# A second level of Strassen's algorithm for one of seven products, and layer-0 row sums on ScalarE

## The chip, the cores and the metric

The kernel runs on one NeuronCore of a Trainium2 chip. TensorE (PE) multiplies matrices into eight PSUM banks, VectorE (DVE) and ScalarE (ACT) work elementwise and empty the banks, GpSimd (POOL) does elementwise work on SBUF alone, and SyncE (SP) issues DMAs. The metric is the device time of the program in microseconds. Three runs of the kernel before gave 1717.29 to 1717.60, median 1717.36.

## The reference

x is 64 batch elements of 256 tokens by 512 features in float32; adj is a 256 x 256 matrix of zeros and ones.

```python
# layer 0
h = relu(layernorm(x))
q, k, v = h @ Wq.T, h @ Wk.T, h @ Wv.T
rel = adj.T * (q @ k.T)                       # per batch element
rel = rel / norm(rel, axis=2, keepdims=True)  # rows over m
x = x + rel @ v
# layer 1
h = relu(layernorm(x))
x = x + (adj @ h) @ weight + bias
```

## The kernel before, in words

Two batch elements make a pair: 512 token rows, held as four chunks of 128 rows. There are 32 pairs, and five input buffers are used in turn. Wq and Wk are multiplied into one matrix M before the pairs start, so a pair needs these products: g (h times M), v (h times Wv), scores (g against h), attend (rel times v), gather (adj times the second h) and mix (times `weight`).

All but the gather use the seven-product (Winograd) form of Strassen's algorithm: each operand is a 2 x 2 grid of blocks, sums of blocks are made by DVE (`left_factors`, lines 158 to 161, and `right_operands`, lines 133 to 136), and seven block products take the place of eight. The products run in the order one, five, six, three, seven, two, four, in three PSUM banks: bank_a takes 1, 6, 7 and 4, bank_c takes 5 and 3, bank_b takes 2. After each product a "take" adds the bank to a block of the result. A first take into g, v or rel is a copy by ACT; all other takes are DVE adds. A block product of g, v or mix is four matmuls of 256 columns, one of the scores four of 128 columns, one of the attend two of 256. An fp32 matmul stands in the trace as two records.

`steady(i)` is the loop body, run for 28 of the 32 pairs; `first_pairs` and `last_pairs` are the ends. It runs in this order on PE: attend of pair i, its seven products alternating with the seven v products of pair i+1 (`attend_and_v`); scores of pair i+1; g of pair i+2 (`project_g`); gather of pair i; mix of pair i. Between products the other engines' work is handed in by "slots": slot n is what is run after the n-th product and its take. On PE, DVE and ACT the program's order is kept as it is written; [...]the slots set each queue's order.

What else matters around the change:

- Layer-0 statistics of pair i+3 (`norm`, lines 248 and 249: two DVE instructions for each chunk) run in the attend slots, then a square root on ACT, two small DVE instructions, and four Relu on ACT (line 260) that write h.
- h is turned in two steps. `place_blocks` issues 16 DMAs on SP's queue (line 299) that permute 32 x 32 blocks from h into the tile `blocks`; then eight DVE transposes (line 309) make ht. In the kernel before they stand in the gather's slots. `sums` are the four DVE operand sums of ht.
- rel is turned likewise. In the slots of g the masks, squares (line 380), root, inverse and scales run, then `place` issues 16 DMAs on SP's queue (line 396) from rel into `placed`, and four DVE transposes (`turns`, line 399, slot 4 of mix) make `turned`. Their sums (`rel_steps`, slot 5 of mix) and those of v (`v_steps`) are the operands of the next attend.
- Layer 1: statistics of the attended x on DVE (`halves`), Relu on ACT, and a split of h into a rounded part (`upper`, ACT, line 499) and the rest (`lower`, DVE, line 503), because the gather runs in the fp32r form, once with each part. POOL adds the bias to x (line 495) and stores each finished pair.

Of the kernel before, what the change touches and what calls it, by code (L numbers as in the profile page):

```python
# [9 lines left out]
F32 = mybir.dt.float32  # L10
# [9 lines left out]
def kernel(  # L20
# [60 lines left out]
    X, H, HL, G, V, R, H2, Y = ({} for _ in range(8))  # L81
# [12 lines left out]
    adj_sb = const.tile([P, NC, N], F32, name="adj_sb")  # L94
# [48 lines left out]

    def run(steps):
        for step in steps:
            step()
# [5 lines left out]
    def left_factors(a, s):  # L152

        v = nc.vector
        steps = [
            lambda: v.tensor_sub(s[0], a(0, 0), a(1, 0)),
            lambda: v.tensor_add(a(1, 0), a(1, 0), a(1, 1)),
            lambda: v.tensor_sub(s[1], a(1, 0), a(0, 0)),  # L160
            lambda: v.tensor_sub(s[2], a(0, 1), s[1]),
        ]
        return {1: a(0, 0), 2: a(0, 1), 3: s[2], 4: a(1, 1), 5: a(1, 0), 6: s[1], 7: s[0]}, steps
# [29 lines left out]

    def winograd(product, take, side={}, early=False):

        for at, step in enumerate(winograd_steps(product, take, early)):
            step()
            run(side.get(at, ()))
# [66 lines left out]


    def ln0(i):

        if i == 0:
            H[i] = blocks.rearrange("p c d e -> p c (d e)")  # L270
        else:
            H[i] = work.tile([P, TC, D], F32, tag="hy", name=f"h_{i}")
        h = H[i]
        chunks, root, end, relu = norm(flat(X[i]))
        return chunks, root, end, [(lambda c=c: relu(h[:, c, :], c)) for c in range(TC)]

# [3 lines left out]
    def transposes_by_matmul(i):  # L280
        h, ht = H.pop(i), new_ht(i)
        for d in range(DC):
            pt = ps_m.tile([P, T], F32, tag="pm", name="pt")
            for half in range(NC):
                for b in range(NB):
                    nc.tensor.transpose(
                        pt[:, ts(half * NB + b, P)], h[:, b * NC + half, ts(d, P)], ident
                    )
            nc.scalar.copy(ht[:, d].rearrange("p h t -> p (h t)"), pt)
        HL[i], sums = left_operands(twice, ht, "hs", i)  # L290
        return sums

# [23 lines left out]
    def project_g(i, side={}):  # L316

        g = work.tile([P, DC, NC, HT_], F32, tag="g", name=f"g_{i}")

        def take(t, k, bank, first):  # L320
            dst = g[:, k * HC : (k + 1) * HC, t, :]
            src = bank.rearrange("p (e t) -> p e t", e=HC)
            if first:
                nc.scalar.copy(dst, src)  # L324
            else:
                nc.vector.tensor_add(dst, src, dst)

        winograd(product_tokens_moving(HL[i], m_right), take, side)
        G[i] = g

    def g_operands(i, tag="ys"):

        g, t = G[i], work.tile([P, 3, HC, HT_], F32, tag=tag, name=f"gt_{i}")
        G[i], steps = right_operands(
            lambda j, k: g[:, j * HC : (j + 1) * HC, k], [t[:, n] for n in range(3)]
        )
        return steps
# [16 lines left out]

    def scores(i, side={}, by_matmul=False):
# [6 lines left out]
        square = work.tile([P, N], F32, tag="square", name=f"square_{i}")  # L362
# [16 lines left out]
        def square_sum(b, k):  # L379
            nc.scalar.activation(square, rel[:, b, k], AF.Square, accum_out=rn[:, b, k : k + 1])  # L380
# [62 lines left out]
    def attend_operands(i):  # L443


        turned, rel = R.pop(i)
        v, t = V.pop(i), work.tile([P, 3, NB, HD], F32, tag="gt", name=f"vt_{i}")
        room = rel.rearrange("p b k m -> p (b k m)")
        left, left_steps = left_factors(
            lambda n, m: turned[:, :, m, n],  # L450
            [room[:, ts(j, HT_)].rearrange("p (b n) -> p b n", b=NB) for j in range(3)],
        )
        right, right_steps = right_operands(
            lambda m, k: v[:, :, m, ts(k, HD)], [t[:, n] for n in range(3)]
        )
        R[i] = left, right
        return right_steps, left_steps

    def attend_and_v(i, side):
# [14 lines left out]
        both = zip(winograd_steps(product, take), winograd_steps(*v_products(i + 1)))  # L474
        for at, (step, v_step) in enumerate(both):
            step()
            v_step()
            run(side.get(at, ()))
# [31 lines left out]
    def gather(i, exact, side={}):  # L510
        h2 = H2.pop(i)
        if exact:
            terms = [(h2[:, s], adjt_r[:, m, :], m) for m in range(NC) for s in range(2)]
        else:
            terms = [(h2, adjt_sb[:, m, :], m) for m in range(NC)]
        y = work.tile([P, DC, NC, NB, P], F32, tag="hy", name=f"yt_{i}")
        for b in range(NB):
            for d0 in range(0, DC, 2):
                pm = ps_m.tile([P, 2, N], F32, tag="pm", name="py")
                for d in range(2):  # L520
                    for n, (left, right, m) in enumerate(terms):
                        nc.tensor.matmul(  # L522
                            pm[:, d, :], left[:, b * NC + m, ts(d0 + d, P)], right,
                            start=(n == 0), stop=(n == len(terms) - 1),
                        )
                nc.scalar.copy(  # L526
                    y[:, d0 : d0 + 2, :, b, :], pm.rearrange("p d (h n) -> p d h n", h=NC)
                )
                run(side.get(b * 2 + d0 // 2, ()))
        Y[i], steps = left_operands(work, y.rearrange("p d h b n -> p d h (b n)"), "ys", i)  # L530
        return steps

    def mix(i, side={}, early=False):
# [10 lines left out]
        winograd(product_weights_moving(Y.pop(i), w_right), take, side, early)  # L544
# [11 lines left out]
    def layer_1(parts):  # L556
# [4 lines left out]
            1: [uppers[0], uppers[1], lowers[0]],  # L561
            2: [relus[2], lowers[1]],
            3: [relus[3], uppers[2], uppers[3]],
# [4 lines left out]
    def before_pairs():  # L568
# [42 lines left out]
        def take(t, k, bank, first):  # L611
# [15 lines left out]
            4: [transpose_wv, end] + relus + [right_steps[3]],  # L627
            5: m_steps[0:3],
# [11 lines left out]
    w_right, w_steps = weight_operands(w_sb, "w")  # L640
    in_order = {EngineType.PE, EngineType.DVE, EngineType.Activation}
# [7 lines left out]
    def pairs(exact):  # L649
        with tc.manual_schedule(engines=in_order):  # L650
            sums = first_pairs(exact)
            for i in range(1, NP - 3):
                if i + 4 < NP:
                    load(i + 4)
                sums = steady(i, exact, sums)
            last_pairs(exact, sums)

    def first_pairs(exact):
# [35 lines left out]
            3: turned2[4:6] + relus[2:4], 4: turned2[6:8], 5: turns[0:2], 6: turns[2:4],  # L694
# [3 lines left out]
            0: sums2[0:1], 1: sums2[1:2], 2: sums2[2:3], 6: sums2[3:4],  # L698
# [6 lines left out]
        if exact:  # L705
# [5 lines left out]
        y_steps = gather(0, exact, {  # L711
            0: turned3[4:8], 1: v_steps[0:1], 2: v_steps[1:3], 3: v_steps[3:4],
        })
        run(y_steps[0:2])
        mix(0, {0: y_steps[2:3], 1: y_steps[3:4], 4: turns, 5: rel_steps})
        return sums3

    def steady(i, exact, sums):
# [4 lines left out]
        stats0, root0, end0, relus0 = ln0(i + 3)  # L723
        stats, root, end, relus, uppers, lowers = ln1(i, exact)
        halves = [stats[b * NC + t] for t in range(NC) for b in range(NB)]
        attend_and_v(i, {
            0: stats0[0:2], 1: stats0[2:4] + [root0], 2: [end0, relus0[0]] + gs[0:2],
            3: relus0[1:2] + gs[2:3], 4: relus0[2:3] + gs[3:4], 5: relus0[3:4] + sums[0:1],
            6: halves[0:2],
        })  # L730
        place_blocks(i + 3)
        masks, squares, norm_root, inverse, scales, place, turns = scores(i + 1, {
            0: halves[2:3], 1: halves[3:4] + [root], 2: [end] + sums[1:2], 3: relus[0:1],
            4: relus[1:2], 5: uppers[0:1], 6: uppers[1:2] + sums[2:4],
        })
        v_steps, rel_steps = attend_operands(i + 1)
# [3 lines left out]
            2: uppers[2:4] + squares[0:2] + v_steps[0:1],  # L740
            3: lowers[2:3] + squares[2:4] + [norm_root],
            4: lowers[3:4] + [inverse] + scales + [place],
            5: v_steps[1:2],
            6: v_steps[2:4],
        })
        turned, sums = transpose_blocks(i + 3)
        y_steps = gather(i, exact, {0: turned[0:3], 1: turned[3:6], 2: turned[6:8]})
        run(y_steps[0:2])
        mix(i, {0: y_steps[2:3], 1: y_steps[3:4], 4: turns, 5: rel_steps})
        return sums  # L750

    def last_pairs(exact, sums):
# [5 lines left out]
        attend_and_v(a, {  # L758
# [14 lines left out]
        gs = g_operands(c, "gt")  # L773
# [13 lines left out]
        attend(c, {n: [stats[n], y_steps[n]] for n in range(TC)}, rn)  # L787
        mix(b, layer_1(parts))
# [39 lines left out]
```

## Time and profile before

| | |
|---|---|
| Median of three runs | 1717.36 us |
| Profiled execution | 1717.2 us, span 1715.1 us |
| PE busy | 1702.2 us, 99% of the span |
| DVE busy | 1360.1 us, 79% |
| ACT busy | 663.3 us, 39% |
| POOL busy | 201.2 us, 12% |
| Granted TensorE clock | 0.999 |

The span runs from the first to the last instruction of the profiled execution; the execution's own time is 2.1 us longer. Busy time is the union of an engine's records. Matmuls overlap one another, so the mean duration of a record (380 ns for 256 columns) is longer than the distance between two records; the chain that ended last gives the distance. A line of the waits reads: engine, tile and line that waited, what released it, microseconds in total, times, and the longest. A line of the groups gives the operation with its operands, how often it ran, then the busy time and the mean duration of one in nanoseconds, then the idle time before it.

### The profile page before, as it was taken

The page shows a single profiled execution, that of the slowest core. Times are in us where ns is not written, and L with a number is a line of the kernel's source. Part 1 is how long each engine was busy: PE and PEld are TensorE (multiplying, and loading weights), DVE is VectorE, ACT ScalarE, POOL GpSimd, SP SyncE. Part 2 cuts the span into 40 slices and gives each one's busy share as a digit, 9 for nine tenths or more (in the row PEclk, how much of TensorE's full clock was granted, in tenths as well). Part 3 has the DMA queues.
Part 4 walks back from the last instruction along what each step waited for, and adds up shares of the span by engine and source line. Part 5 has one row for each costly group of instructions (what it writes and reads, how often), then busy time and mean ns, then how long its engine had stood idle before and what let it go on. Part 6 is the DMA issues. An engine that isn't in the chain of part 4 may idle for free.

```text
span 1715.1 us, 24952 instructions
## 1 busy us (share of the span) xinstructions
PE 1702.2 (99%) x9170; PEld 1518.2 (89%) x9170; DVE 1360.1 (79%) x2672; ACT 663.3 (39%) x1387; POOL 201.2 (12%) x167
## 2 busy tenths in 40 slices
PE   9999999999999999999999999999999999999998
PEld 7979998989898999889898989998889989899986
DVE  6778888878888888888787888888888888887655
ACT  4434433444333344334443333443343433334331
POOL 0011100111101111001111011110011110011111
PEclk9999999999999999999999999999999999999999
DMA  7423333233332233332233322333322334222011
GB/s 239 65 33 80 77 86 76 51 59 80 81 86 66 45 74 77 86 77 56 53 81 80 87 67 48 71 76 85 78 59 49 81 80 87 68 53 41 28 24 63
DMA packets 425972, 122.34 MB, mean 71 GB/s; under 512 B 398064, under 2 KB 399344, under 8 KB 425840
## 3 DMA queue, kind: packets, MB, share of 16 engines
q1 hardware_dynamic: 413248, 80.28, 25.1%
q0 software_dynamic: 8432, 32.51, 5.0%
q10 hardware_dynamic: 4160, 7.87, 1.3%
q8 instruction: 74, 1.21, 0.3%
q14 instruction: 58, 0.48, 0.1%
HBM read 38.27 MB, written 33.55 MB: 42 GB/s over the span
## 4 chain that ended last, share of the span: by engine, by line
PE 96%; DVE 3%; ACT 0%; DMA 0%; issue 0%; ACTq 0%; DVEq 0%
PE bank_a L217 25%; PE bank_c L217 13%; PE bank_a L205 13%; PE py L522 7%; PE bank_a L229 7%; PE bank_b L217 7%; PE bank_c L205 6%; PE bank_a L465 6%; PE bank_c L229 3%; PE bank_b L205 3%; PE bank_c L465 3%; PE bank_b L229 2%; PE bank_b L465 1%; DVE st L248 1%; PE pu L430 0%; DMA wk_sb<-in_L_gnn_Wk_dram 0%
## 5 line engine op out<-in xcount | busy, mean ns | idle before, releaser
L346 ACT COPY v<-bank_a 128x512 f32<-128x512 f32 x96 | 56.2, 586 | 676.6 <-PE bank_a L217 676.6
L495 POOL TENSOR_TENSOR x_ring<-x_ring,bias_bc 128x512 f32<-128x512 f32 x128 | 176.3, 1396 | 822.6 <-DVE rel L372 548.8
L248 DVE BATCH_NORM_STATS2 st<-x_ring 128x6 f32<-128x512 f32 x256 | 171.5, 670 | 0.4
L539 DVE TENSOR_TENSOR x_ring<-bank_a,x_ring 128x512 f32<-128x512 f32 x128 | 88.2, 689 | 57.9 <-PE bank_a L217 57.9
L522 PE MATMUL py<-adjt_r,h 128*128 128x256 f32 x1024 | 130.4, 285 | 0.0
L522 PEld LDWEIGHTS py<-adjt_r,h 128*128 128x128 f32 x1024 | 123.9, 189 | 1.6
L217 PE MATMUL bank_a<-w_t,ys 128*128 128x256 f32 x512 | 121.3, 380 | 1.7 <-DVE x_ring L539 1.7
L217 PE MATMUL bank_a<-wv_t,hs 128*128 128x256 f32 x512 | 121.0, 379 | 0.0
L205 PE MATMUL bank_a<-hs,m_t 128*128 128x256 f32 x512 | 121.0, 379 | 0.0
L260 ACT ACTIVATE h2c<-x_ring,nb,rs 128x512 f32<-128x512 f32 x128 | 100.6, 810 | 32.6 <-DVE h L503 25.9
L217 PEld LDWEIGHTS bank_a<-w_t,ys 128*128 128x128 f32 x512 | 95.7, 190 | 17.3 <-DVE x_ring L539 3.0
L217 PEld LDWEIGHTS bank_a<-wv_t,hs 128*128 128x128 f32 x512 | 97.4, 190 | 13.1
L205 PEld LDWEIGHTS bank_a<-hs,m_t 128*128 128x128 f32 x512 | 97.4, 190 | 13.1
L546 POOL DMA_DIRECT2D out_dram<-x_ring x31 | 24.0, 773 | 671.2 <-issue 489.2
L503 DVE TENSOR_TENSOR h<-h2c,h 128x512 fp32r<-128x512 f32 x128 | 91.1, 711 | 5.6 <-ACT h L499 5.6
L526 ACT COPY yt<-py 128x512 f32<-128x512 f32 x128 | 75.1, 587 | 47.2 <-PE py L522 47.2
L260 ACT ACTIVATE h<-x_ring,nb,rs 128x512 f32<-128x512 f32 x124 | 91.0, 806 | 1.5 <-DVE nb L257 1.5
L309 DVE STREAM_TRANSPOSE ht<-blocks 128x256 f32<-128x256 f32 x248 | 84.8, 407 | 1.4 <-DMA blocks<-h 1.4
L539 DVE TENSOR_TENSOR x_ring<-bank_c,x_ring 128x512 f32<-128x512 f32 x64 | 44.2, 691 | 46.1 <-PE bank_c L217 46.1
L472 DVE TENSOR_TENSOR x_ring<-bank_a,x_ring 128x512 f32<-128x512 f32 x116 | 79.4, 685 | 1.3 <-PE bank_a L465 1.3
L499 ACT CAST h<-h2c 128x512 fp32r<-128x512 f32 x128 | 75.3, 616 | 0.0
L324 ACT COPY g<-bank_a 128x512 f32<-128x512 f32 x96 | 56.2, 586 | 43.2 <-PE bank_a L205 41.1
(175 smaller groups left out, 3669.4 us busy)
## 6 DMA issues: line engine op xcount, KB each, us to landing
blocks<-h SPq DMA_DIRECT2D x496, 64.0 KB, 2.3
out_dram<-x_ring POOLq DMA_DIRECT2D x31, 1024.0 KB, 4.7
x_ring<-in_x_dram SPq DMA_DIRECT2D x28, 1024.0 KB, 5.3
placed<-rel SPq DMA_DIRECT2D x496, 32.0 KB, 2.0
x_ring<-in_x_dram ACTq DMA_DIRECT2D x4, 1024.0 KB, 5.3
wq_sb<-in_L_gnn_Wq_dram SPq DMA_DIRECT2D x4, 256.0 KB, 5.0
wk_sb<-in_L_gnn_Wk_dram ACTq DMA_DIRECT2D x4, 256.0 KB, 6.3
wv_sb<-in_L_gnn_Wv_dram ACTq DMA_DIRECT2D x1, 1024.0 KB, 5.4
```

The lines of the kernel that those rows point to most:

```text
L205: nc.tensor.matmul(bank[:, e * HT_ : (e + 1) * HT_], right[n][:, d, ts(e, P)], left[n][:, d, :], start=(start and e == 0 and d == 0), stop ...
L217: nc.tensor.matmul(bank[:, b * HD : (b + 1) * HD], left[n][:, d, ts(b, P)], right[n][:, d, :], start=(start and b == 0 and d == 0), stop=( ...
L229: nc.tensor.matmul(bank[:, ts(b, P)], right[n][:, d, ts(b, P)], left[n][:, d, ts(b, P)], start=(start and b == 0 and d == 0), stop=(d == H ...
L248: nc.vector.bn_stats(st[:, c, :], src[:, c, :])
L260: nc.scalar.activation(dst, src[:, c, :], AF.Relu, bias=nb[:, c : c + 1], scale=rs[:, c : c + 1])
L309: nc.vector.transpose(ht[:, d, half].rearrange("p (b n) -> p b n", b=NB), by_half[:, :, half, d])
L465: nc.tensor.matmul(bank[:, ts(b, HD)], left[n][:, b], right[n][:, b], start=(start and b == 0), stop=True, skip_group_check=True,)
L472: nc.vector.tensor_add(dst, bank.rearrange("p (b e) -> p b e", b=NB), dst)
L495: nc.gpsimd.tensor_tensor(xt[:, c, :], xt[:, c, :], bias_bc, ALU.add)
L503: nc.vector.tensor_sub(dst[:, 1, c, :], whole_h[c], dst[:, 0, c, :].bitcast(F32))
L522: nc.tensor.matmul(pm[:, d, :], left[:, b * NC + m, ts(d0 + d, P)], right, start=(n == 0), stop=(n == len(terms) - 1),)
L539: nc.vector.tensor_add(xt[block], bank.rearrange("p (b e) -> p b e", b=NB), xt[block])
```

## The change

1. **A second level for one product.** In g, v and mix of the steady pairs, product 2 (which went to bank_b) is itself computed by seven products. Its blocks, 256 x 256 each, are cut once more into 128 x 128, so that seven matmuls of 128 columns stand in place of four of 256. They run in one further bank, `bank_d`, in three 128-column regions, as four groups: 1 and 5 behind product six; 6 and 3 behind three; 7 and 2 behind seven; 4 behind a "spacer". DVE adds the regions to the result: two adds behind group 1, one behind group 2, two behind group 3 (the last with 256 columns), one behind group 4.
2. **Spacers.** Group 4 follows something else on PE: in v the attend product that stands there anyway, in g the first of four gather steps, in mix the first attend product of the next pair.
3. **Operands of the second level.** Twelve 128-column right sums are made once (`second_right`); for each pair four left sums of h (`second_of_h`) and four of y (`second_of_y`). In `left_factors` the sum goes to a fourth room if one is given.
4. **Layer-0 statistics by ScalarE** in the steady pairs (`norm_by_scalar`): a Copy with a row sum and a Square with a bias and a row sum for each chunk, with three small DVE instructions and the root between.
5. **Rooms.** The sums of v (`vt`) lie in the tile `blocks` (`spare_blocks`); the squares' unused output goes to `placed`; the input adj shares the room of `placed`.
6. **Moves.** The transposes of h go from the gather's slots to slots 2 to 5 of g; the sums of ht from the end of `attend_and_v` and the scores to slots 1 to 3 of `attend_and_v`; the sums of g to slots 4 to 6; two of the v sums and two of the rel sums (`late`) into slots 0 and 1 of the next `attend_and_v`. At the ends: `transpose_wv` one slot later, the v sums of pair 1 from the gather into mix, two y sums of the last pairs from attend into mix, and the layer-1 steps of `layer_1` in another order.

```diff
+    def second_level(matmul, add):
+        bank = ps_m.tile([P, 512], F32, tag="pm", name="bank_d")
+        at_a, at_b, at_c = (bank[:, ts(r, P)] for r in range(3))
+        def group_1():
+            matmul(at_a, 1, True)
+            matmul(at_c, 5, False)
+            add(0, 0, at_a)
+            add(1, 1, at_c)
+        def group_2():
+            matmul(at_a, 6, False)
+            matmul(at_c, 3, False)
+            add(0, 1, at_a)
+        def group_3():
+            matmul(at_a, 7, False)
+            matmul(at_b, 2, False)
+            add(1, 1, at_a)
+            add(0, None, bank[:, P : 3 * P])
+        def group_4():
+            matmul(at_a, 4, False)
+            add(1, 0, at_a)
+        return group_1, group_2, group_3, group_4
+    def two_level_steps(product, take, matmul, add, spacer):
+        one, five, six, three, seven, _, four = winograd_steps(product, take)
+        groups = second_level(matmul, add)
+        return [
+            lambda: run([one]),
+            lambda: run([five]),
+            lambda: run([six, groups[0]]),
+            lambda: run([three, groups[1]]),
+            lambda: run([seven, groups[2]]),
+            lambda: run([spacer, groups[3]] if spacer else [groups[3]]),
+            lambda: run([four]),
+        ]
...
+    def norm_by_scalar(src, scratch):
...
+        def total(c):
+            nc.scalar.activation(scratch[:, c, :], src[:, c, :], AF.Copy, accum_out=sm[:, c : c + 1])
+        def mean():
+            nc.vector.tensor_single_scalar(sm, sm, -1.0 / D, op=ALU.mult)
+        def square(c):
+            nc.scalar.activation(
+                scratch[:, c, :], src[:, c, :], AF.Square, bias=sm[:, c : c + 1],
+                accum_out=sq[:, c : c + 1],
+            )
...
+    def spare_blocks():
+        room = blocks.rearrange("p c d e -> p (c d e)")
+        return [room[:, ts(n, 512)].rearrange("p (a b) -> p a b", a=2) for n in range(3)]
...
-        v, t = V.pop(i), work.tile([P, 3, NB, HD], F32, tag="gt", name=f"vt_{i}")
+        v, t = V.pop(i), spare_blocks()
...
-    def steady(i, exact, sums):
+    def steady(i, exact, sums, attends, late, first_done):
...
-        attend_and_v(i, {
-            0: stats0[0:2], 1: stats0[2:4] + [root0], 2: [end0, relus0[0]] + gs[0:2],
-            3: relus0[1:2] + gs[2:3], 4: relus0[2:3] + gs[3:4], 5: relus0[3:4] + sums[0:1],
-            6: halves[0:2],
+        attend_and_v(i, first_done, attends, {
+            0: late[0:3] + totals[0:2], 1: late[3:4] + totals[2:4] + [mean] + sums[0:1],
+            2: row_squares[0:2] + sums[1:3], 3: row_squares[2:4] + [root0, end0] + sums[3:4],
+            4: relus0[0:2] + gs[0:1], 5: relus0[2:4] + gs[1:3], 6: gs[3:4] + halves[0:1],
         })
...
-            2: uppers[2:4] + squares[0:2] + v_steps[0:1],
-            3: lowers[2:3] + squares[2:4] + [norm_root],
-            4: lowers[3:4] + [inverse] + scales + [place],
-            5: v_steps[1:2],
-            6: v_steps[2:4],
-        })
+            2: uppers[2:4] + squares[0:2] + turned[0:2],
+            3: lowers[2:3] + squares[2:4] + [norm_root] + turned[2:4],
+            4: lowers[3:4] + [inverse] + scales + [place] + turned[4:5],
+            5: turned[5:8],
+        }, second=True, spacer=y_products[0])
+        v_steps, rel_steps = attend_operands(i + 1)
+        run_steps(y_products[1:], {0: v_steps[0:1], 1: v_steps[1:2]})
         run(y_steps[0:2])
-        mix(i, {0: y_steps[2:3], 1: y_steps[3:4], 4: turns, 5: rel_steps})
-        return sums
+        y_second = second_of_y(i)
+        attends = attend_steps(i + 1)
+        mix(i, {
+            0: y_steps[2:3], 1: y_steps[3:4] + y_second[0:2], 2: y_second[2:4],
+            4: turns, 5: rel_steps[0:2],
+        }, spacer=attends[0])
+        return sums, attends, v_steps[2:3] + rel_steps[2:4] + v_steps[3:4]
```

## The prediction

> **What bounds the kernel now.** I read the page's busy times and chain first, then the chain in order of time over one steady pair (a pair is 2 of the 64 batch elements; the loop body runs for 28 of the 32), then PE's waits, then the same pair on DVE and SP.
>
> ```profile
> PE 1702.2 (99%) x9170; PEld 1518.2 (89%) x9170; DVE 1360.1 (79%) x2672; ACT 663.3 (39%) x1387; POOL 201.2 (12%) x167
> PE 96%; DVE 3%; ACT 0%; DMA 0%; issue 0%; ACTq 0%; DVEq 0%
> PE bank_a L217 <- DVE x_ring L539: 1.7, 3, 0.9
> PE bank_c L217 <- DVE yt L159: 1.4, 1, 1.4
> ```
>
> PE is the bound, and it waits for hardly anything (all its listed waits add to about 7 us). The time is PE's work, so work taken off PE pays in full, and any new PE wait costs in full. From the chain, in order of time (start, duration, record):
>
> ```profile
> 820.60 0.86 PE bank_a L465 x4
> 823.19 0.89 PE bank_a L229 x8
> 829.44 1.73 PE bank_a L205 x8
> 838.08 1.73 PE bank_b L205 x8
> 841.53 3.77 PE py L522 x32
> ```
>
> An fp32 matmul is two records. 256 columns take 1.727/8 = 215.9 ns a record, 128 columns 0.893/8 = 111.7 ns. One pair on PE: 21 weight products x 1.727, 7 score products x 0.893, 7 attend products x 0.864 and the gather 3.77 = 52.3 us.
>
> DVE and SP of the same pair (start, duration):
>
> ```profile
> 852.60 0.69 DVE L539 TENSOR_TENSOR x_ring<-bank_c,x_ring 128x512 f32<-128x512 f32 x1 [1.38 <-PE bank_c L217]
> 854.33 0.69 DVE L539 TENSOR_TENSOR x_ring<-bank_a,x_ring 128x512 f32<-128x512 f32 x1 [1.03 <-PE bank_a L217]
> 854.93 1.41 DVE L399 STREAM_TRANSPOSE turned<-placed 128x256 f32<-128x256 f32 x4
> 856.27 0.65 DVE L539 TENSOR_TENSOR x_ring<-bank_b,x_ring 128x512 f32<-128x512 f32 x1
> 816.31 11.88 SPq L299 DMA_DIRECT2D blocks<-h  x16
> 841.26 11.34 SPq L396 DMA_DIRECT2D placed<-rel  x16
> blocks<-h SPq DMA_DIRECT2D x496, 64.0 KB, 2.3
> placed<-rel SPq DMA_DIRECT2D x496, 32.0 KB, 2.0
> ```
>
> The row at 854.33 takes product "seven" of the mix; right behind it DVE makes the four `turned` blocks of the next attend. PE first reads them at 857.58, after products "two" and "four". The first block is ready at 854.93 + 0.40 = 855.33: a margin of 2.25 us. The 16 `placed` DMAs start at 841.26 and, at 0.709 apiece plus 2.0 to land, end near 853.9, 1.0 before the turns.
>
> Rows for prices:
>
> ```profile
> L326 DVE TENSOR_TENSOR g<-bank_b,g 128x512 f32<-128x512 f32 x32 | 22.1, 689 | 10.2 <-PE bank_b L205 10.2
> L372 DVE TENSOR_TENSOR rel<-bank_b,rel 128x256 f32<-128x256 f32 x32 | 13.6, 425 | 14.5 <-PE bank_b L229 14.5
> L260 ACT ACTIVATE h<-x_ring,nb,rs 128x512 f32<-128x512 f32 x124 | 91.0, 806 | 1.5 <-DVE nb L257 1.5
> L380 ACT ACTIVATION_READ_ACCUMULATOR square<-rel 128x1 f32 x128 | 24.0, 187 | 0.0
> ```
>
> **What the skill says.** The Trainium skill, "TensorE: Matmul & The Clock Gate", section Back-to-back issue gap: N/2.4 + 2.5 ns. Two passes give 111.7 ns at N = 128, exactly the trace, and 218 at 256 against 215.9. "VectorE: DVE Perf Modes", section The TRN2 errata, prices an fp32 tensor_tensor at (N+151)/0.96 ns: 691 and 424 agree with 689 and 425; for N = 128, which the trace lacks, 291. "ScalarE: Activation LUTs", section What ACT_TABLE_LOAD costs: 186 + 0.833 N ns and 93 for each pointer operand: 799 for the Relu, measured 806. "PSUM — Partial Sum Buffer", section PSUM bank collisions raise a hardware error, has two engines take turns on one bank; no trace here shows a collision, but it is why the second level must run in groups, with DVE's adds between them and PE waiting.
>
> **The change, part by part.** (a) PE. One product of eight records (1.727) becomes seven 128-column matmuls, 14 x 111.7 = 1.564: 0.163 saved. In the loop g, v and mix have it: 0.49 a pair; with one more v behind the loop, 13.8 us in all. This is the whole gain.
>
> (b) DVE, a pair: three takes of 689 go, twelve adds of 291 and three of 425 come: +2.7. Second left operands, 8 x 291: +2.3. The layer-0 statistics, 4 x (670+182), go: -3.4; a scaled mean, +0.2. Net +1.8 on 42.5, still 83% of 53 us, so DVE is not the bound as a sum; where its queue stands at each PE need decides.
>
> (c) ACT: four Copies (613+187) and four Squares with a bias pointer (706+187): +6.8 on 20.7, off the path as a sum. In the attend slots two of them (about 1.5 with overlap) stand between v copies that come every 2.59 us: hidden with 0.5 to spare. But DVE's variance and reciprocal now sit in its queue waiting for ACT's fourth square and root, and the takes of "seven" behind them. Laying the order out with the rows' durations, DVE leaves these 0.2 us before the take would hold PE: hidden, and every 0.1 beyond costs 0.1 a pair (2.8 us).
>
> (d) The spacer in mix. Group 4 needs group 3's add, so attend's first product is put between, directly behind group 3. That product's stationary operand is `turned`. PE now wants it 0.447 us (four small matmuls) after "seven", not 3.45 (two products): 3.01 earlier. DVE does two more adds, about 0.20 + 0.34 in back-to-back spacing, before it turns: 0.54 later. The margin becomes 2.25 - 3.01 - 0.54 = **-1.3 us: a PE stall in each of 28 pairs**. Both matmuls of the product need a turn, but the second is 0.33 behind and PE spends 0.43 on the first. After a stall the first weight load is exposed: the stall at 850.57 made the next product 1.83 instead of 1.73, so +0.1.
>
> (e) Behind it stands a second floor. From "seven" of g to the spacer PE now runs 0.447+0.942+0.223+1.727+2.826+5.180+0.447+1.727+0.447+1.727+0.447 = 16.1 us. `place` came 3.2 after that "seven"; two more adds make it 3.7, and 15 x 0.709 + 2.0 + 0.40 for one turn give 16.75. So the DMAs alone would hold PE about 0.6; now hidden under the 1.3 of (d).
>
> (f) Groups 4 of v and g. From "seven": DVE starts 0.2 later, takes 0.60, adds 0.20 + 0.42, signal 0.04: 1.46. PE has 0.447 + 0.864 (attend product) in v, 0.447 + 0.942 (one gather step) in g: stalls of 0.15 and 0.07. In g, ACT's copy of "five" stands behind a relu that waits for DVE; I put 0.15 on "three".
>
> (g) `vt` moves into `blocks`. Its last reader is attend's last product, so `place_blocks` starts there (about 16 us into the stretch, not 10.5), and needs 15 x 0.742 + 2.3 = 13.4: blocks at about 29.5. The turns of h, moved from the gather to g's slot 2, come at about 30.0: 0.5 to spare on DVE and 1.2 more before PE. Costs nothing while this holds. On SP's queue they end near 28, before `place` at 36.7; POOL's queue (bias adds, the store) is not moved. The squares that now write into `placed` stand ahead of `place` on ACT anyway, and their region's last readers, the turns, are half a pair behind: nothing. Moved too, at nothing while DVE has room: two `v` and two `rel` steps (2.2 us) behind the next v's "one", needed only by attend "six" two products later.
>
> (h) Outside the loop: the shift of transpose_wv and of operand steps may remove the 1.7 and 1.4 waits above: -3 us. The once-made right operands, 12 x 291 = 3.5, lie beside full PE slots.
>
> **Sum.** Per pair -0.49 + 1.3 + 0.1 + 0.15 + 0.07 + 0.15 = +1.28; x 28 = +36; less 0.16 and 3: **+33 us**. The profiled execution took 1717.2 (span 1715.1), within 0.2 of the median 1717.36: 1750.
>
> **Rivals.**
> 1. *The DMAs of `placed` bind the spacer* (e later than d). Speaks for it: only 0.5 us between the two; every delay of DVE in g's slots 3 and 4 shifts `place`. Against: the issue rate is steady in the trace. One microsecond late makes the stall 1.8: +14, 1764.
> 2. *DVE's or ACT's queue holds PE elsewhere*: statistics on ACT slower than their price, or a 128-column add dearer than 291. Slacks in (c) and (f) are 0.2 and below zero, so 0.06 more on each of some 20 small operations costs 0.4 to 0.5 a pair: 1763; 0.2 more, 1810.
> 3. *Shorter stalls*: a 128-column add between 172 (the 128x4 rows) and 291 and quicker signals: stall 1.0, (f) gone, net +0.6: 1734.
> 4. *Faster*: the spacer does not wait. Place: first attend product in mix. It decides at a stall of 0.49 us, below which the gain in (a) wins; with none, 1717.2 - 13.8 - 3 = 1700. It needs the turns 1.3 earlier, or PE already that late for another reason; against it speak both (d) and (e), each enough alone.
> 5. *PE gains nothing*, if seven weight loads with 128 columns each ran slower: the scores (111.7 a record, a new weight each) speak against; then 1764.
>
> **How the numbers follow.** Likeliest, 0.5: 1750, 1738 to 1762. Rival 1: 0.17; rival 2: 0.16; rival 3: 0.10; rival 5: 0.02; rival 4: 0.04; within 0.2% of before, 0.01 (the place where 3 and 4 meet). Leaving out rival 4, the dear end of 2 and the far tails gives 1733 to 1782. Three runs spread 0.3 us, so 0.2% (3.4 us) is about what can be told from no change: faster 0.04, same 0.01, slower 0.95.
>
> **What would show it.** PE's waits should list the attend product (its first bank in mix) behind DVE `turned`, 28 times, about 1.3 each, or behind DMA `placed` if rival 1 holds. The small products should space at 111.7 a record and PE's busy time fall by 14. Waits on the second-level bank should be near 0.15. PE idle of about 50 us would confirm the sum; no such wait, or the turns ahead of the take of "seven", would make it wrong; ht waiting for DMA `blocks` over 1 us would mean (g) failed.

## The result and the profile after

Four runs of the changed kernel gave 1760.72 to 1761.66 us, median 1760.95, against 1717.36 before. The ratio is 1.0254, with a 95% interval of 1.0237 to 1.0272. The change makes the kernel 43.6 us slower. The profiled execution took 1761.66 us, with a span of 1759.4; before, the span was 1715.1, so the two traces differ by 44.3 us, at the same granted clock (0.999).

The page of the kernel after, busy times and the shares of the chain that ended last:

```profile
PE 1711.0 (97%) x9680; PEld 1525.2 (87%) x9680; DVE 1393.6 (79%) x3141; ACT 791.4 (45%) x1835; POOL 192.2 (11%) x167
PE 92%; DVE 4%; SPq 1%; issue 1%; DMA 1%; ACT 0%; DVEq 0%; ACTq 0%
```

PE is still the bound, but it now stands idle for 48.4 us of the span (before: 12.9), and DVE carries 4% of the chain. PE's busy time rose by 8.8 us although its work fell. A record of 256 columns lasts 379 ns and the next one starts 216 ns behind it, so a wait of up to 0.16 us leaves no gap between the records, and a longer one shows 0.16 too short; that part counts as busy. So neither the busy times nor the list of waits gives the whole loss. The list of PE's waits, kernel after:

```profile
PE bank_a L612 <- DVE turned L546: 36.8, 28, 1.4
...
PE bank_d L487 <- DVE ys L169: 0.3, 1, 0.3
```

One wait comes in every one of the 28 pairs, 1.31 us each: the first attend product of the next pair, which is the spacer in mix, waits for the transposes that make `turned`. Of the second-level bank the list has a single wait, 0.3 us.

How long is one pair? The first and last start of attend's product in bank_b give it (29 attends, 28 intervals). Kernel before, then kernel after (durations min/median/max, then first and last start):

```profile
L465 PE MATMUL bank_b<-v,turned x116: 378/379/380, 137.4 to 1603.6; 128*128 128x256 f32 x116
```

```profile
L612 PE MATMUL bank_b<-v,turned x116: 379/379/382, 138.3 to 1650.5; 128*128 128x256 f32 x116
```

(1603.6 - 137.4)/28 = 52.36 before and (1650.5 - 138.3)/28 = 54.01 after: +1.65 a pair, +46 in the loop. The head became 0.9 longer, and the tail (span less the last start) went from 111.5 to 108.9. The sum is +44.3, the whole difference. (The last start is that of the fourth record of its product, 0.65 us behind the first, so every period in this document is 0.02 too long; differences between kernels are not touched.)

Where the 1.65 sits is seen in the chain in order of time over one pair of the kernel after (start, duration, record):

```profile
887.77 0.45 PE bank_d L487 x4
...
895.16 0.49 PE bank_d L487 x2
...
915.39 0.43 PE bank_d L440 x2
...
925.47 0.62 PE bank_d L487 x4
...
930.03 0.48 DVE x_ring L703
...
930.64 0.07 DVE x_ring L491
...
930.84 0.41 DVE x_ring L491
931.25 0.36 DVE turned L546
...
931.75 1.10 PE bank_a L612 x4
932.85 0.22 PE bank_d L487 x2
```

The first line is a group of four small records that waits for nothing: 0.45. A group 4 with nothing to wait for takes 0.22, as in the last line. Against these, group 4 of v takes 0.49, group 4 of g 0.43, and group 1 of mix 0.62. From 930.03 on PE is out of the chain: DVE takes product "seven", adds the two regions of group 3, makes the first turned block, and only then the spacer runs. It stands in the chain with 1.10, where an attend product is 0.86.

DVE, PE and SP at that place (start, duration, line, operation, count, and in brackets the idle time before and what ended it):

```profile
930.03 0.69 DVE L703 TENSOR_TENSOR x_ring<-bank_a,x_ring 128x512 f32<-128x512 f32 x1 [1.28 <-PE bank_a L276]
930.64 0.61 DVE L491 TENSOR_TENSOR x_ring<-bank_d,x_ring 128x128 f32<-128x128 f32 x2
931.17 1.41 DVE L546 STREAM_TRANSPOSE turned<-placed 128x256 f32<-128x256 f32 x4
931.75 1.10 PE L612 MATMUL bank_a<-v,turned 128*128 128x256 f32 x4 [1.31 <-DVE turned L546]
896.59 11.61 SPq L406 DMA_DIRECT2D blocks<-h  x16
917.73 10.39 SPq L543 DMA_DIRECT2D placed<-rel  x16
```

The `placed` DMAs were issued from 917.73, 10.39/16 = 0.65 us apiece, so by estimate the last landed near 917.73 + 15 x 0.65 + 2.0 = 929.5. The turns began 1.7 later and did not wait for it. DVE was idle for 1.28 us before the take of "seven", and in the last 0.5 of these the blocks lay ready; its order held the turns behind the take.

The rows that answer to the price rows of before, from the groups of the kernel after, shapes kept apart, and from its DMA issues:

```profile
L449 DVE TENSOR_TENSOR g<-bank_d,g 128x128 f32<-128x128 f32 x140 | 36.5, 278 | 20.5 <-PE bank_d L440 20.5
L340 ACT ACTIVATE h<-x_ring,sm 128x512 f32<-128x512 f32 x112 | 79.5, 714 | 0.0
L340 ACT ACTIVATION_READ_ACCUMULATOR h<-x_ring,sm 128x1 f32 x112 | 21.4, 191 | 0.0
blocks<-h SPq DMA_DIRECT2D x496, 64.0 KB, 2.3
placed<-rel SPq DMA_DIRECT2D x496, 32.0 KB, 2.0
```

The new operations cost what the prediction priced: 278 ns for a 128-column add (priced 291), 714 for the Square (706), 191 for the accumulator read (187). The landing times are those of before.

**The short waits.** The timeline of PE, kernel after, at the three places with a few tenths too much:

```profile
895.16 0.49 PE L487 MATMUL bank_d<-wv_t,ht 128*128 128x128 f32 x2
915.34 0.49 PE L440 MATMUL bank_d<-ht,m_t 128*128 128x128 f32 x2
925.60 0.49 PE L487 MATMUL bank_d<-w_t,ys 128*128 128x128 f32 x2
```

Two such records without a wait stand in the timeline as 0.38 or 0.39. By the starts of the single records of group 4 of v: the last record before it began at 894.780, the next was due 0.216 later, at 894.996, and began at 895.162; that is a wait of 0.17. The second record then began 0.213 behind the first, not 0.112: another 0.10, which is the weight load of the first (see the last section). In g the wait is 0.11 (due at 915.227, begun at 915.337) and in mix 0.07 (due 925.532, begun 925.604), and in both the second record again comes 0.213 behind the first. So each wait, however short, costs 0.10 on top. The sums are 0.27 in v, 0.21 in g and 0.17 in mix.

The ledger for one pair: -0.49 of saved matmul time (a), +1.31 for `turned`, +0.24 for the spacer's longer run, +0.27, +0.21 and +0.17. It sums to +1.71; the period says +1.65, so 0.06 a pair is left over. The 0.24 is what the list leaves out of this wait (0.16) and a later second record (0.08).

### The profile page after: what moved, and what is told of

It reads as the page before. It is cut to its first block, busy times and chain, and to the rows that moved or that the text cites. A ratio compares the mean times of both kernels' runs of the same rounds, so it can differ in the third digit from the quotient of the medians.

```text
span 1759.4 us, 27004 instructions
## 1 busy us (share of the span) xinstructions
PE 1711.0 (97%) x9680; PEld 1525.2 (87%) x9680; DVE 1393.6 (79%) x3141; ACT 791.4 (45%) x1835; POOL 192.2 (11%) x167
## 4 chain that ended last, share of the span: by engine, by line
PE 92%; DVE 4%; SPq 1%; issue 1%; DMA 1%; ACT 0%; DVEq 0%; ACTq 0%
PE bank_a L276 24%; PE bank_c L276 12%; PE bank_a L264 12%; PE py L675 7%; PE bank_a L288 6%; PE bank_c L264 6%; PE bank_a L612 6%; PE bank_d L487 5%; PE bank_c L288 3%; PE bank_c L612 3%; PE bank_d L440 3%; PE bank_b L288 2%; PE bank_b L612 1%; DVE x_ring L703 1%; DVE x_ring L491 1%
## 5 line engine op out<-in xcount | busy, mean ns | idle before, releaser
L647 POOL TENSOR_TENSOR x_ring<-x_ring,bias_bc 128x512 f32<-128x512 f32 x128 | 167.4, 1327 | 841.9 <-ACT h2c L319 841.9
L675 PE MATMUL py<-adjt_r,h 128*128 128x256 f32 x1024 | 136.5, 287 | 0.0
L264 PEld LDWEIGHTS bank_a<-hs,m_t 128*128 128x128 f32 x512 | 95.1, 190 | 11.8
L307 DVE BATCH_NORM_STATS2 st<-x_ring 128x6 f32<-128x512 f32 x144 | 96.4, 670 | 0.4
L416 DVE STREAM_TRANSPOSE ht<-blocks 128x256 f32<-128x256 f32 x248 | 93.5, 417 | 3.6 <-DMA blocks<-h 3.3
L354 ACT ACTIVATE h<-x_ring,nb,rs 128x512 f32<-128x512 f32 x112 | 82.0, 803 | 12.4 <-DVE nb L351 12.4
L536 ACT ACTIVATE rel<-rel,rn 128x256 f32<-128x256 f32 x124 | 52.9, 497 | 68.5 <-DVE rn L533 68.5
L340 ACT ACTIVATE h<-x_ring,sm 128x512 f32<-128x512 f32 x112 | 79.5, 714 | 0.0
```

The costliest lines, as they stand in the source:

```text
L264: nc.tensor.matmul(bank[:, e * HT_ : (e + 1) * HT_], right[n][:, d, ts(e, P)], left[n][:, d, :], start=(start and e == 0 and d == 0), stop ...
L307: nc.vector.bn_stats(st[:, c, :], src[:, c, :])
L416: nc.vector.transpose(ht[:, d, half].rearrange("p (b n) -> p b n", b=NB), by_half[:, :, half, d])
L647: nc.gpsimd.tensor_tensor(xt[:, c, :], xt[:, c, :], bias_bc, ALU.add)
L675: nc.tensor.matmul(pm[:, d, :], left[:, b * NC + m, ts(d0 + d, P)], right, start=(n == 0), stop=(n == len(terms) - 1),)
```

## The experiments

All seven kernels compute the whole of the reference. E1 to e4 differ from the changed kernel by the edit shown, e5 and e7 from e3, e6 from e5. "Period" is the time of one pair, from the first and last start of attend's product in bank_b as above. The kernel before, run beside them, gave medians of 1717.64 (e1 to e4) and 1717.73 (e5 to e7). E2 and e4 have one run each.

### e1: everything but the second level

```diff
-        for at, (step, v_step) in enumerate(zip(steps, v_steps_by_two_levels(i + 1))):
+        for at, (step, v_step) in enumerate(zip(steps, winograd_steps(*v_products(i + 1)))):
...
-        }, second=True, spacer=y_products[0])
+        })
...
-        }, spacer=attends[0])
+        })
```

(With it go `second_of_h`, `second_of_y` and their slots, and the attend product returns to its place.)

> The changed kernel without its second level: product two runs whole again, no spacers, and the second left sums are not made; the statistics on ACT, the sums of v in the tile blocks and all moved steps stay. Theory (the loss is PE waiting behind the second level's own chain): a pair returns to 52.33 us and the ends keep their gain of about 2.5, so 1714 to 1716 us, with no PE wait on turned. Rival (the moves, the statistics on ACT or the lent room cost part of the 1.7 us a pair): 1725 us or more, with PE or DVE waits behind ACT or the blocks DMAs.

Measured: 1713.68 us (1713.12 to 1714.59), ratio 0.9977 with interval 0.9967 to 0.9987; period 52.33. From its page:

```profile
PE 1702.0 (99%) x9170; PEld 1517.6 (89%) x9170; DVE 1261.4 (74%) x2488; ACT 800.9 (47%) x1835; POOL 203.2 (12%) x167
```

PE's waits have neither `turned` nor a second-level bank. What follows: the statistics on ACT, the shared rooms and all the moves together cost nothing in the loop (52.33 against 52.36) and gain 4 us in all. Of the 2.9 us between the two traces, 1.1 is in the loop and 1.8 at the ends. DVE waits for the `blocks` DMAs nine times here, 10.3 us in all, but PE doesn't. The whole loss is made by the second level, and 52.33 is the base to measure it from.

### e2: two turns ahead of the take of "seven"

```diff
-            4: turns, 5: rel_steps[0:2],
+            3: turns[0:2], 4: turns[2:4], 5: rel_steps[0:2],
```

> Two of the four turns of rel go one slot earlier on DVE's queue, ahead of the take of seven in mix; nothing else changes. Theory (DVE's chain of take and adds ahead of the turns makes the 1.3 us): the wait on turned falls to 0.2 or less, but the take and the adds are then late by the turns, so group 4 of mix waits about 0.5 with an exposed weight load; 1.5 - 0.8 saved, about 1740 us. Rival (the placed DMAs bind just behind the chain, 0.5 to 0.8 us): DVE waits for placed, PE still waits 0.5 or more for turned, and the time stays above 1748 us.

Measured: 1743.59 us; period 53.38. PE's waits, then DVE's wait on the DMAs, kernel e2:

```profile
PE bank_d L487 <- DVE x_ring L491: 7.9, 26, 0.4
PE bank_a L612 <- DVE turned L546: 7.4, 12, 1.4
...
DVE turned L546 <- DMA placed<-rel: 32.1, 27, 2.5
```

Its chain in order of time, the end of the row of DMA issues and what follows it:

```profile
919.50 0.61 SPq L543
...
920.15 1.90 DMA placed<-rel
...
922.18 0.77 DVE turned L546 x2
922.95 0.58 DVE x_ring L703
923.53 0.54 DVE x_ring L491 x2
924.06 0.14 issue
924.20 0.46 PE bank_d L487 x2
```

With the turns out of the way 17 us come back and PE's wait on `turned` falls from 36.8 to 7.4 us. So DVE's order was the first cause. But the result lies between the two expectations, because the second floor is right behind: the turns now wait for the last of the `placed` DMAs in 27 pairs (1.2 us each), DVE's take of "seven" stands behind the turns, and group 4 waits for that. SP's queue is in the chain here, which it was not at this place in the changed kernel.

### e3: the next v's first product as the spacer of mix

```diff
-            if at or not first_done:
-                step()
-            v_step()
+            step()
+            if at or not first_done:
+                v_step()
...
-        }, spacer=attends[0])
+        }, spacer=v_next[0])
```

(`v_next` are the v steps of pair i+2; the attend product goes back behind product "four".)

> The spacer of mix is product one of the next v, whose operand is ready long before, in place of attend's first product, which returns behind four. Theory: the 1.3 us wait and the 0.24 us of exposed weight load vanish from each of 28 pairs, 43 us: about 1718 us, that is no better than before, since the waits of group 4 in v and g and of group 1 in mix (0.27, 0.21, 0.17 us in the trace) eat the 0.49 us gained. Rival (PE would find another wait a little later, in DVE's or ACT's queue): above 1730 us with a new wait in the list.

Measured: 1718.08 us (1716.78 to 1721.19), ratio 1.0004 with interval 0.9995 to 1.0013; period 52.50. The wait on `turned` is gone from the list. The chain in order of time of e3 keeps the three small ones (group 4 of g, group 1 of mix, group 4 of v):

```profile
894.41 0.43 PE bank_d L440 x2
904.58 0.62 PE bank_d L487 x4
926.66 0.49 PE bank_d L487 x2
```

This spacer multiplies Wv with a block of ht that was turned in the g stretch of the round before, so it needs nothing that mix is still making. The period closes: 52.33 - 0.49 + 0.27 + 0.21 + 0.17 = 52.49. Against the changed kernel it gives back 42.9 us, all of it for one product in another place. The second level then just pays for its own small waits.

### e4: no spacer in mix

```diff
-        }, spacer=attends[0])
+        })
```

(The attend product goes back to its place here too.)

> No spacer in mix: group 4 follows group 3 directly, and attend's first product returns behind four. Theory: group 4 needs the take of seven and two adds of DVE, 1.46 us after seven, of which group 3 itself covers 0.45, so PE waits 1.0 with 0.25 of exposed weight load in place of 1.54: about 1753 us. Rival (only the turns are late, group 4's own chain is short): about 1718 us as with the other spacer.

Measured: 1751.45 us; period 53.66. PE's waits, kernel e4:

```profile
PE bank_d L487 <- DVE x_ring L491: 26.9, 28, 1.0
```

Without a spacer group 4 waits for the add of group 3, 0.96 us in each pair. That is dear, but 0.35 a pair cheaper than the spacer of the change (53.66 against 54.01). The spacer was put in to cover a wait of 0.96 us and brought one of 1.31.

### e5: group 4 behind "four", and the second sums of y first

On top of e3:

```diff
-            lambda: run([spacer, groups[3]] if spacer else [groups[3]]),
-            lambda: run([four]),
+            lambda: run([spacer] if spacer else []),
+            lambda: run([four, groups[3]]),
...
-            0: y_steps[2:3], 1: y_steps[3:4] + y_second[0:2], 2: y_second[2:4],
+            0: y_steps[2:3], 1: y_second[0:2] + y_steps[3:4], 2: y_second[2:4],
```

> On top of the v spacer in mix: group 4 runs behind product four in v, g and mix, and the first two second sums of y go ahead of the last first-level sum on DVE. Theory (what was left of the loss is group 4 coming 0.15 us before DVE's adds, and group 1 of mix before its sum, each with an exposed weight load: 0.27 + 0.21 + 0.17 us a pair in the trace): 18 us less than with the v spacer alone, 1700 us, 1 per cent under the kernel before, and no PE wait on bank_d. Rival (DVE's queue is so full that the wait appears elsewhere): 1712 us or more with a new line in PE's waits.

Measured: 1700.80 us (1699.93 to 1701.74), ratio 0.9903 with interval 0.9889 to 0.9917: faster than both kernels. From the page and from the chain in order of time of e5 (group 4 of g, then group 1 of mix, then group 4 of mix and of v):

```profile
PE 1685.0 (99%) x9680; PEld 1520.2 (90%) x9680; DVE 1394.5 (82%) x3141; ACT 792.8 (47%) x1835; POOL 192.3 (11%) x167
```

```profile
886.38 0.22 PE bank_d L440 x2
894.53 0.44 PE bank_d L487 x4
902.77 0.22 PE bank_d L487 x2
919.01 0.22 PE bank_d L487 x2
```

Every second-level group now has its unhindered length. The period is (1589.0 - 138.5)/28 = 51.80; the base of e1 less the saved matmul time is 52.33 - 0.49 = 51.84. PE's busy time is now 17.2 us below that of before; 13.8 of this is the saved work, the rest was not followed up. DVE's work takes the same time as in the changed kernel (1394.5 against 1393.6); only the order is different, on PE and on DVE.

### e6: e5 with the layer-0 statistics on DVE again

```diff
-        totals, mean, row_squares, root0, end0, relus0 = ln0_by_scalar(i + 3)
+        totals, root0, end0, relus0 = ln0(i + 3)
+        row_squares = []
```

(and without `[mean]` in slot 1.)

> The version with the late group 4, but layer 0's statistics of the steady pairs go back to DVE's two instructions a chunk, in the same slots; nothing else changes. Theory: DVE then has 3.2 us more in the attend stretch, which is already nearly full (about 0.2 us of slack), so takes and the sums of g come late and PE waits in the attend and score products for DVE: 1735 to 1745 us. Rival (the statistics on ACT were no condition, since DVE is 83 per cent busy at most): within 3 us of the version with the late group 4.

Measured: 1735.53 us (1735.36 to 1735.92), ratio 1.0105 with interval 1.0089 to 1.0121; period 53.05. From its page and its list of PE's waits:

```profile
PE 67%; DVE 30%; issue 2%; SPq 1%; ACT 1%; DMA 0%; DVEq 0%
```

```profile
PE bank_a L288 <- DVE rel L516: 16.1, 28, 1.5
```

DVE is busy for 85% of the span only, and yet 30% of the chain is DVE's: in the attend stretch its queue falls behind PE, and PE waits for it at the end of the scores. The listed wait is 0.58 us a pair; the period grew by 1.25, the rest in waits too short for the list. Moving the statistics to ACT is worth 34.7 us in this arrangement (1735.53 - 1700.80), though without the second level (e1) the same move leaves the loop as long as before. What was tried is these slots; another order of DVE's work, with the statistics spread over the stretches where DVE has room, was not.

### e7: e3 with the second sums of y first, alone

On top of e3:

```diff
-            0: y_steps[2:3], 1: y_steps[3:4] + y_second[0:2], 2: y_second[2:4],
+            0: y_steps[2:3], 1: y_second[0:2] + y_steps[3:4], 2: y_second[2:4],
```

> The v spacer in mix, with only the order of DVE's sums of y changed: two second sums go ahead of the last first-level sum. Theory: group 1 of mix no longer waits for its second sum (0.17 us a pair in the trace): 1713 us. Rival (the 0.17 us is the weight load behind a bank change and stays): 1718 us as before.

Measured: 1714.13 us (1713.39 to 1717.69), ratio 0.9981 with interval 0.9974 to 0.9988; period 52.33. A swap of two entries in one slot takes out the 0.17 of group 1 of mix: 52.50 - 0.17 = 52.33. What is left to e5 is 13.3 us (1714.13 - 1700.80), and group 4's two waits say 28 x (0.27 + 0.21) = 13.4.

## Why the prediction was right, and where its terms were off

The forecast was 1750 us, slower, with `turned` as the cause; 1760.95 came. The mechanism was right, and it was 11 us too low because small terms were mis-sized. By its steps:

(a) **The saved matmul time.** Right. Four small records run in 0.44 to 0.45, as 4 x 111.7 ns says, and e5, where nothing waits, shows the whole gain of 0.49 a pair (51.84 expected from e1, 51.80 measured). Rival 5 is out.

(b) **DVE's sum.** Nearly right and of no consequence. The page has +33.5 us; less twelve once-made sums of about 0.285 that is 30.1 over 28 pairs, +1.1 a pair instead of +1.8. E1's page splits it: the second level took +132.2 (4.6 a pair after the once-made sums, priced 5.0), the rest of the change -98.7 (-3.5, priced -3.2). Adds in a row overlap (in the pair shown one begins 0.197 behind another that lasts 0.280), which a sum of durations doesn't see. That the net came so close is partly luck: two effects that the prediction didn't have cancel, sums that were slowed by 1.8 us a pair before and others by 1.9 after (last section). DVE did not become the bound.

(c) **Statistics on ACT.** Right: hidden. ACT grew by 128.1 us, 4.6 a pair and not 6.8; its operations in a row overlap as well (one Square begins at 888.295 and the next at 889.012, 0.72 later, where a Square with its accumulator read lasts 0.724 + 0.190). E1 has the same statistics and a period no longer than before. So rival 2 did not come from ACT or from dearer adds; e6 shows it was close by, had the statistics stayed on DVE.

(d) **The spacer in mix.** Right in cause, place and count (28 times), and the stall of 1.3 is listed as 1.31. But the list counts from the end of the record before. By the starts of single records, the record before the spacer began at 930.164; the spacer's first was due at 930.276 and began at 931.750, 1.47 late, and its second record came 0.29 behind it instead of 0.216. So the product ends 1.55 late, where the step had 1.3 + 0.1.

DVE's record of the first turned block ends at 931.604, 1.33 behind the due time, as the step says. PE begins to load this block as its weight at 931.719, 0.115 later, and from there to the second record it is 0.321, 0.105 more than the spacing. The 0.105 is the exposed load, which the step has as 0.1. The Trainium skill, "TensorE: Matmul & The Clock Gate", section LDWEIGHTS (loading the stationary operand), prices a load at columns/1.2 ns: 107 for 128 columns, and the next load of this product begins 0.108 behind the first. The term left out is the 0.115 between DVE's record and PE's load.

(e) **The second floor.** It didn't hold the changed kernel: DVE has no wait for `placed` in the whole run. In the pair shown the transfers were issued at 0.65 us apiece, and by estimate the last landed near 929.5. A first turn could have been done at about 929.9 and its load begun at about 930.0, before the 930.17 at which it was due. So rival 1 fell. The 0.709 apiece of the step came from one pair: the row of 16 issues lasts 10.39 to 11.55 us over the pairs of the kernel before and 10.38 to 11.84 in the changed kernel. With the longest row the last transfer would land near 930.9, still before the turns at 931.17. But it is a floor as the step says: e2, which takes away (d), runs onto it at once.

(f) **Group 4 of v and g.** The waits were right: 0.15 predicted for v and 0.17 measured, 0.07 for g and 0.11 measured. What failed is the cost of a wait: each takes 0.10 more for the exposed weight load, so 0.27 and 0.21. The step has this cost in (d) and leaves it out here. The 0.15 on g's "three" behind ACT's copy did not come: in the chain that product begins as soon as the group ahead of it ends. And one wait was not foreseen at all: group 1 of mix needs the second sum of y, which stood behind a 128 x 512 sum of y in DVE's queue; 0.07 late, 0.17 dear. E7 shows the cause by swapping the two.

(g) **Rooms and moves.** Right: nothing for PE. The `blocks` transfers, issued from 896.59, land near 896.59 + 15 x 0.726 + 2.3 = 909.8, and in the whole run DVE waited for them once. E1 has all of it and no loss, though DVE waits for `blocks` there nine times.

(h) **The ends.** Right in direction, half the size: -3 predicted, and the tail fell by 2.6 but the head grew by 0.9, -1.7 in all. In e1 it is -1.8. The two waits of 1.7 and 1.4 are gone in both.

The sum: predicted +1.28 a pair, the ledger has +1.71. The difference of 0.43 is +0.15 in (d), +0.12 and +0.14 in (f), +0.17 for group 1 of mix, and -0.15 for "three". Times 28 that is 12 us. Measured by the period, the loop has 10.2 more than forecast (46.0 against 35.8), and the ends bring 1.4 less (-1.7 against -3.2): together 11.6, as between the traces (44.3 against a forecast of 32.7).

Rival 4 said what the kernel would take if the spacer didn't wait: 1700. Its condition was not met by the change, and e3 shows that it was not enough (1718.08), since the three small waits use up the gain; with these gone too, e5 takes 1700.80.

## What to carry to other kernels

A filler put into a bound engine's queue to cover a wait must itself need nothing recent: ask of each candidate when its operands are ready, and price the filler's own wait against the one it covers (here 1.31 against 0.96). A wait of 0.07 us on PE cost 0.17, for a weight load came out into the open; such waits don't appear in the list of waits or in the busy time, but in the chain, as a group of records that is longer than its like (0.49 against 0.22). Where the gain is 0.49 us in a period of 52, look at each new consumer of a fresh sum before judging the idea: the same arithmetic was 2.5% slower in one order and 1% faster in another.

## What the runs showed of the hardware that was not expected

- A wait of 0.07 to 0.17 us on PE was followed each time by a second record 0.213 us behind the first, where 0.112 is the spacing without a wait. The records of the weight loads show where it goes. Without a wait a load begins one matmul ahead of its own: the one at 894.020 belongs to the matmul at 894.130. Behind the wait in v the first load and its matmul begin together, at 895.160 and 895.162, and the next load 0.109 later. So the first load of 0.1 us lies in the open, where otherwise it runs under the matmul ahead. No run changes the load alone, so this is read from the records and not tried.
- The row of 16 `placed` issues takes 10.4 us in some pairs and up to 11.5 (before) or 11.8 (after) in others, with the same 32 KB and the same code. Why is open; no run was made for it.
- Two of the new 128-column sums take over four times their price (291). Of the sums of h for the second level, DVE runs two at 281 to 284 ns and two far slower, in every pair. From the groups, shapes kept apart, of the kernel after:

```profile
L170 DVE TENSOR_TENSOR hs<-hs,ht 128x128 f32<-128x128 f32 x29 | 36.9, 1272 | 1.0
L171 DVE TENSOR_TENSOR hs<-ht,hs 128x128 f32<-128x128 f32 x29 | 35.2, 1215 | 1.0
```

POOL's two bias adds begin at 904.39 in the pair shown and last 2.54 us; these two sums begin at 904.50 and 905.84. In the kernel before, two other sums had such means, and no longer do:

```profile
L160 DVE TENSOR_TENSOR hs<-ht 128x512 f32<-128x512 f32 x32 | 49.4, 1545 | 0.1
L133 DVE TENSOR_TENSOR vt<-v 128x512 f32<-128x512 f32 x29 | 48.9, 1685 | 0.0
```

The same sums take 722 and 692 ns in the changed kernel. The Trainium skill, "SBUF — State Buffer", section SBUF: two separate sides, says that a DVE operation with two SBUF inputs and a GpSimd operation that reads SBUF exclude each other for the whole instruction, the one that starts later waiting. The traces agree: in the pair shown POOL's adds end at 905.652 and 906.936 and the two sums at 905.803 and 907.086, each 0.15 later. E6, where DVE's queue stands differently, shows the order at work, in its timelines of DVE and POOL:

```profile
891.86 0.29 DVE L170 TENSOR_TENSOR hs<-hs,ht 128x128 f32<-128x128 f32 x1
892.18 1.25 DVE L171 TENSOR_TENSOR hs<-ht,hs 128x128 f32<-128x128 f32 x1
892.02 2.55 POOL L647 TENSOR_TENSOR x_ring<-x_ring,bias_bc 128x512 f32<-128x512 f32 x2 [21.82 <-ACT h2c L319]
```

The sum of L170 begins 0.16 before POOL's first add and takes 0.29; the next begins 0.16 after it and takes 1.25. Over e6 the first has a mean of 330 ns, against 1334 in e5. So the moves took 1.8 us a pair off DVE and the new sums put 1.9 back, at a place where DVE had room. No run moves POOL's adds themselves.
